# Two transformer layers on one core: half of a sequence's rows turned in 32x32 squares by VectorE and moved in SBUF, where TensorE turned them before

## The chip, the cores and the metric

The kernel runs on one core of a Trainium2 chip. The metric is the device time of one execution in microseconds (us). Four compute engines matter here: TensorE (PE, matmuls and transposes), VectorE (DVE), ScalarE (ACT) and GpSimd (POOL). SyncE (SP) issues most of the DMAs; ACT and POOL issue some as well. Matmul results land in PSUM, which the kernel uses as eight banks; everything else is in SBUF, with 128 partitions.

## The reference, cut to what matters

Two sequences (B=2) of 512 tokens with 512 features go through two layers, each an attention block and a feed-forward block. A residual is added and the rows are normalized after each block. The change lies between the first two blocks.

```python
# layer 0, attention: every fourth query head reads a memory M, normalized by z
q_sel = (elu(q) + 1)[:, :, ::4, :]                     # 8 heads of 128
num = einsum('bshd,hde->bshe', q_sel, M)
den = einsum('bshd,hd->bsh', q_sel, z)[..., None] + 1e-6
output = repeat(num / den, 4, axis=2).reshape(b, s, 4096) @ Wo.T
x = layernorm(x + output)                              # (M_new, z_new are not returned)
# layer 0, feed-forward: quantized, truncated to int8 twice; w_gate, w_up are ternary
gate, up = (x / 128) @ w_gate.T, (x / 128) @ w_up.T
inter_q = trunc(clip(silu(gate) * up * 128, -128, 127)).astype(int8)
x = layernorm(x + trunc(clip(inter_q @ w_down.T * 128, -128, 127)).astype(int8))
# layer 1: softmax attention, then a SwiGLU block of inner width 1376
x = layernorm(x + attention(x));  x = layernorm(x + swiglu(x))
```

## The kernel before

A sequence is cut into four tiles of 128 tokens; a tile has its tokens in the 128 partitions and 512 features along the row. The first block works in that layout. The feed-forward block contracts over the features, so it needs each sequence transposed: features in partitions, 512 tokens along the row, in four blocks of 128 features. It is needed in two parts, `xh` (a copy rounded to the matmul's input format, fp32r) and `xl` (what the rounding left), because each product of the block is taken with both parts.

The stage that the change touches is the loop over the eight tiles of both sequences, first (0,0) to (0,3) and then (1,0) to (1,3); step i handles `order[i]`. A step does this:

- `read(b, t)`: eight matmuls on PE (L557, tile `po`, one per head, each into its own PSUM bank). ACT takes the head's denominator from the last column (L561, `den`). DVE takes the reciprocal of four denominators at once (L565). The first three heads are scaled by ACT into SBUF tiles `y` (L570), which POOL adds up (L574). Heads 3 to 7 are scaled and added to the rows `x` by DVE (L579). Last, POOL adds the sum of the three to `x` (L586). A bank is free again when its head has been scaled.
- In the middle of `read`, `norm_a0(i - 1)` normalizes the tile before: statistics on DVE (L138, L140), a power on POOL (L146, L147), an offset on DVE (L664), and the final scaling on ACT (L665). So tile t is fully normalized in the middle of the step after it.
- `check_up`, `total`, `verdict`: steps that find whether the up weights are ternary, with a small matmul `pf_up` (L224) near the end.

After step 5 and after step 6, `block(k)` is called twice each: it transposes block k of all four tiles of the first sequence on PE (L275, four transposes of 128x128 into one PSUM bank `pt_f`), ACT copies the bank to `xh` (L280), and DVE subtracts to give `xl` (L281). The second sequence goes another way already: `turn_squares` lets DVE turn each normalized tile square by square, each square left where it stands (L671, a stream transpose into `squares`), and later `move_squares` sends each square to its place by 16 DMAs (L294): 9 from SP's queue, 4 from POOL's, 3 from ACT's. `split(1, xt1)` then makes `xh` and `xl` from the moved tile `xt_f`.

The order of instructions on PE, ACT, DVE and SP is set by a scheduler with a cost model when the program is built; `issue_after` ties single instructions to others. POOL's order alone is that of the code. PSUM tiles come from one pool of eight banks in turn, so a matmul waits for the reader of the tile eight places earlier. The large SBUF tiles of the stage come from pools: `pair_tile` gives one of four slots of 128x2x512 in pool `wop` (tag `wo`), which held the output weights until their sum was taken, and `xtp` has two slots of 128x4x512.

After the loop, the feed-forward block starts with the first sequence (L735), then the second.

Of the kernel before, what the change touches and what calls it, by code (L numbers as in the profile page):

```python
# [10 lines left out]
F32 = mybir.dt.float32  # L11
F32R = mybir.dt.float32r
# [7 lines left out]
P = 128  # L20
B, S, HID = 2, 512, 512
NT = S // P
NK = HID // P
# [16 lines left out]
def kernel(  # L40
# [19 lines left out]
    nc = tc.nc  # L60
# [6 lines left out]
    xtp = ctx.enter_context(tc.tile_pool(name="xtp", bufs=2))  # L67
# [14 lines left out]
    def psum(name):  # L82
        return ps.tile([P, 512], F32, tag="mm", name=name)


    xs = [[], []]
# [172 lines left out]
            wds.append(wd)  # L259
        return wds  # L260

    def split(b, xt=None):


        hi = xtp.tile([P, NK, S], F32, tag="xt", name=f"xh_{b}").bitcast(F32R)
        los = [pair_tile(f"xl_{b}_{i}").bitcast(F32R) for i in range(2)]
        his = [hi[:, k, :] for k in range(NK)]
        los = [los[k // 2][:, k % 2, :] for k in range(NK)]

        def block(k):  # L270
            h, l = his[k], los[k]
            if xt is None:
                rows = psum(f"pt_f0{b}_{k}")
                for t in range(NT):
                    nc.tensor.transpose(rows[:, ts(t, P)], xs[b][t][:, ts(k, P)], ident)  # L275
            else:
                rows = xt[:, :, k, :]
                h, l = (u.rearrange("p (t q) -> p t q", t=NT) for u in (h, l))
            return (
                nc.scalar.copy(h, rows),  # L280
                nc.vector.tensor_sub(l, rows, h.bitcast(F32)),  # L281
            )

        return his + los, block

    def move_squares(squares, xt):


        src = squares.rearrange("p t (k i) -> p (t k) i", k=NK)
        dst = xt.rearrange("p t k i -> p (t k) i")  # L290
        for i in range(P // SQ):
            for j in range(P // SQ):
                eng = nc.gpsimd if i == j else nc.scalar if i == (j + 2) % 4 > 0 else nc.sync
                dma = eng.dma_start(dst[ts(j, SQ), :, ts(i, SQ)], src[ts(i, SQ), :, ts(j, SQ)])  # L294
                if eng is nc.sync:
                    last = dma
        return last
# [4 lines left out]
    def pair_tile(name):  # L302
        return wop.tile([P, 2, HID], F32, tag="wo", name=name)
# [7 lines left out]
    def units(tile):  # L311
        return [tile[:, i, :] for i in range(tile.shape[1])]
# [66 lines left out]
    with tc.tile_pool(name="a0w", bufs=1) as a0w, tc.tile_pool(name="a0", bufs=2) as a0:  # L379
        wq = []  # L380
        for h in range(NH):
            if h % 2 == 0:
                two = query_tile(f"wq{h}").rearrange("p a (k d) -> p a k d", k=NK)
            w = two[:, h % 2]
# [163 lines left out]
        def read(b, t, between):  # L548

            x = xs[b][t]  # L550
            ys, steps = [], []
            for h0 in range(0, NH, 4):
                four = []
                den = small.tile([P, 4], F32, tag="den", name=f"den_{b}_{t}_{h0}")
                for j in range(4):
                    po = psum(f"po0_{b}_{t}_{h0 + j}")
                    nc.tensor.matmul(  # L557
                        po, qs[b][h0 + j][:, ts(t, P)], mw[:, h0 + j, :],
                        start=True, stop=True,
                    )  # L560
                    nc.scalar.activation(  # L561
                        den[:, j : j + 1], po[:, LAST:], AF.Identity, bias=den_eps
                    )
                    four.append(po)
                nc.vector.reciprocal(den, den)  # L565
                for j in range(4):
                    d = den[:, j : j + 1]
                    if h0 + j < LENT:
                        y = a0.tile([P, HID], F32, tag="y", name=f"y_{b}_{t}_{j}", bufs=3)
                        nc.scalar.activation(  # L570
                            y[:, :LAST], four[j][:, :LAST], AF.Copy, scale=d
                        )
                        if ys:
                            nc.gpsimd.tensor_add(  # L574
                                ys[0][:, :LAST], ys[0][:, :LAST], y[:, :LAST]
                            )
                        ys.append(y)
                    else:
                        steps.append(nc.vector.scalar_tensor_tensor(  # L579
                            x[:, :LAST], four[j][:, :LAST], d, x[:, :LAST], ALU.mult, ALU.add  # L580
                        ))
            between(steps)
            if (b, t) == order[-1]:
                steps.append(nc.vector.tensor_add(x[:, :LAST], x[:, :LAST], ys[0][:, :LAST]))
            else:
                nc.gpsimd.tensor_add(x[:, :LAST], x[:, :LAST], ys[0][:, :LAST])  # L586
            return steps
# [68 lines left out]
        def norm_a0(i, steps):  # L656

            b, t = order[i]
            with tc.issue_after(steps[1].ins):
                stats = layernorm_stats(xs[b][t], f"a0{b}_{t}")  # L660
            with tc.issue_after(steps[-1].ins):
                mv, rstd = stats
                off = small.tile([P, 1], F32, tag="off", name=f"off_{i}")
                nc.vector.tensor_scalar(off, mv[:, 0:1], rstd, -1.0, ALU.mult, ALU.mult)  # L664
            nc.scalar.activation(xs[b][t], xs[b][t], AF.Identity, bias=off, scale=rstd)  # L665

        x2 = []

        def turn_squares(i):
            b, t = order[i]  # L670
            nc.vector.transpose(squares[:, t, :], xs[b][t])  # L671

        for i, (b, t) in enumerate(order):
            steps = read(b, t, lambda steps: norm_a0(i - 1, steps) if i else None)
            for _ in range((1, 1, 1, 1, 1, 1, 0, 0)[i]):
                check_up(*checks.pop(0))
            if i == 5:
                tot_up = total(counts_up[0], "up")
            elif i == 6:
                flag_up, eff_up = verdict(tot_up, sc_up, "up")  # L680
            if i == 5:
                parts, block = split(0)
                x2.append(parts)
                squares = xtp.tile([P, NT, HID], F32, tag="xt", name="squares")
            if i in (5, 6):
                for k in range(2):
                    block(2 * (i - 5) + k)
            if i > NT:
                turn_squares(i - 1)
        norm_a0(len(order) - 1, steps)  # L690
        turn_squares(len(order) - 1)


# [10 lines left out]
        ]  # L704

    xt1 = fp.tile([P, NT, NK, P], F32, tag="it11", name="xt_f01", bufs=1)
    moved = move_squares(squares, xt1)
    wdp = ctx.enter_context(tc.tile_pool(name="wdp", bufs=1))
    with tc.issue_after(moved.ins):
        wds = down_weights(wd0_in, "0")  # L710
    with tc.tile_pool(name="f0", bufs=2) as f0:
# [134 lines left out]

        for c in range(LEAD - 2):
            up(0, c, [cut_off[f"f00_{c - 2}"]] if c > 1 else ())
        parts, block = split(1, xt1)
        x2.append(parts)  # L850
        moved = [ins for k in range(NK) for ins in block(k)]
        for c in range(LEAD - 2, LEAD):
            up(0, c, moved)
        for c in range(LEAD):
# [607 lines left out]
```

## Time and profile before

| | us |
|---|---|
| median of 3 runs | 459.4 |
| the runs | 459.14, 459.40, 459.92 |
| the profiled execution | 459.37 |
| its span in the trace | 457.6 |
| around the span | 1.77 |
| PE busy in the span | 449.9 |

The profile is of one execution. Its span runs from the first to the last instruction; the time outside it is the difference to that execution's own time. A row of a timeline gives the start from the span's start, the busy time of the group, the engine, the line of the kernel, the operation, output and inputs by name, shapes, a count, and in brackets the idle time before it and what ended it. Starts of neighbouring rows are more exact than durations on PE, since matmuls are pipelined and their ends are modelled.

### The profile page before, as it was taken

To read this page: it belongs to the slowest core of one execution; us is meant where nothing else is said; L and a number is where in the kernel's file an instruction comes from. 1 tells how busy PE (TensorE), PEld (TensorE's weight loads), DVE (VectorE), ACT (ScalarE), POOL (GpSimd) and SP (SyncE) were. 2 spreads that over 40 slices of the span, in tenths; PEclk is the share of its full clock that TensorE was granted. 3 is DMA by queue.
4 is the path that set the end of the run, shared out by engine and by line. 5 is a ranking of instruction groups with operands and counts; after the bars stand their busy time and mean duration, and the time that the engine had idled before them with its cause. 6 is when DMAs were issued, how large, how long until landed. Compare 5 with 4: busy or idle time off the path is not lost.

```text
span 457.6 us, 5879 instructions
## 1 busy us (share of the span) xinstructions
PE 449.9 (98%) x1929; PEld 338.0 (74%) x1929; DVE 339.5 (74%) x665; ACT 270.2 (59%) x514; POOL 110.5 (24%) x149
## 2 busy tenths in 40 slices
PE   8999999999999999999999999999999999999995
PEld 8887754344588888888766578888888888888884
DVE  4966757667867888847978899795656778998632
ACT  4778995556567975567748544564755658442101
POOL 0300206565550069101362332000000000050101
PEclk9999999999999999999999999999999999999999
DMA  8999980000038101131585500000000000001001
GB/s 293 392 267 313 178 319 1 0 3 0 2 51 238 55 3 48 47 93 38 199 323 92 94 0 2 0 0 1 0 1 0 1 1 0 1 23 46 34 37 47
DMA packets 28693, 37.14 MB, mean 81 GB/s; under 512 B 16304, under 2 KB 17200, under 8 KB 28656
## 3 DMA queue, kind: packets, MB, share of 16 engines
q1 hardware_dynamic: 23216, 30.13, 19.2%
q0 software_dynamic: 1984, 5.77, 6.8%
q10 hardware_dynamic: 3456, 0.75, 0.8%
q8 instruction: 22, 0.36, 0.3%
q14 instruction: 15, 0.12, 0.1%
HBM read 32.45 MB, written 2.10 MB: 75 GB/s over the span
## 4 chain that ended last, share of the span: by engine, by line
PE 92%; DVE 3%; issue 2%; DMA 1%; ACT 1%; SPq 0%; POOL 0%; POOLq 0%; DVEq 0%
PE pm L1252 17%; PE po L557 10%; PE pq L502 9%; PE pg_f L735 9%; PE pu_f L735 9%; PE pc L1252 8%; PE pdm L1340 8%; PE pd_f L794 4%; PE pdc L1340 4%; PE pqk L1063 3%; PE pv L1080 2%; PE pot L1129 2%; PE po L1146 2%; PE psc L1019 2%; PE pmw L543 2%
## 5 line engine op out<-in xcount | busy, mean ns | idle before, releaser
L557 PE MATMUL po<-mw,q 128*128 128x512 f32 x128 | 57.1, 599 | 0.7 <-ACT den L561 0.4
L557 PEld LDWEIGHTS po<-mw,q 128*128 128x128 f32 x128 | 22.9, 189 | 33.4 <-issue 18.6
L146 POOL TENSOR_TENSOR rstd_f<-mv_f,ln_eps 128x1 f32<-128x1 f32 x15 | 4.4, 295 | 170.8 <-DVE mv_f L1355 130.2
L1252 PE MATMUL pm<-r,ugu 128*128 128x512 f32 x152 | 37.7, 389 | 0.0
L1252 PE MATMUL pm<-r,it_early 128*128 128x512 f32 x144 | 36.6, 392 | 0.0
L1252 PEld LDWEIGHTS pm<-r,ugu 128*128 128x128 f32 x152 | 28.5, 188 | 5.9
L170 ACT ACTIVATE ta_f<-y_f,below_half 128x512 int8<-128x512 f32 (+1 forms) x22 | 15.8, 720 | 27.2 <-DVE y_f L158 26.9
L1252 PEld LDWEIGHTS pm<-r,it_early 128*128 128x128 f32 x144 | 27.0, 188 | 6.0 <-issue 0.5
L579 DVE SCALAR_TENSOR_TENSOR x<-po,den,x 128x511 f32<-128x511 f32 x40 | 29.8, 745 | 2.1
L1262 DVE SCALAR_TENSOR_TENSOR ev_q<-pm,ev_q 128x512 f32<-128x512 f32 x27 | 18.5, 686 | 14.2 <-PE pm L1252 12.0
L574 POOL TENSOR_TENSOR y<-y,y 128x511 f32<-128x511 f32 x16 | 21.1, 1320 | 25.5 <-PE po L557 20.6
L761 DVE SCALAR_TENSOR_TENSOR it_f<-tb_f,ta_f 128x512 fp32r<-128x512 int16 (+1 forms) x22 | 15.2, 690 | 13.8 <-ACT tb_f L171 13.8
L735 PE MATMUL pg_f<-xh,tu 128*128 128x512 f32 x88 | 24.4, 399 | 0.0
L1261 ACT ACTIVATE ev_q<-pc 128x512 f32<-128x512 f32 x27 | 16.0, 594 | 14.1 <-PE pc L1252 14.0
L735 PE MATMUL pg_f<-xl,tu 128*128 128x512 f32 x88 | 23.6, 389 | 0.0
L735 PE MATMUL pu_f<-xh,tu 128*128 128x512 f32 x88 | 23.5, 389 | 0.0
L735 PE MATMUL pu_f<-xl,tu 128*128 128x512 f32 x88 | 23.5, 389 | 0.0
L1142 ACT ACTIVATE x<-x,off_f,rstd_f 128x512 f32<-128x512 f32 x7 | 5.7, 816 | 27.7 <-POOL off_f L1141 27.7
L561 ACT ACTIVATE den<-po,den_eps 128x1 f32<-128x1 f32 x64 | 13.9, 277 | 12.8 <-PE po L557 12.7
L349 POOL TENSOR_SCALAR td<-wd,inv_down 128x512 fp32r<-128x512 f32 x11 | 20.1, 1847 | 1.6 <-DVE inv_down L206 1.6
L794 PE MATMUL pd_f<-td,it_f 128*128 128x512 f32 x88 | 20.3, 389 | 0.0
L1252 PE MATMUL pc<-r,ugu 128*128 128x512 f32 x72 | 19.3, 390 | 0.0
(368 smaller groups left out, 1142.7 us busy)
## 6 DMA issues: line engine op xcount, KB each, us to landing
gu<-in_gu SPq DMA_DIRECT2D x20, 512.0 KB, 6.9
wd<-in_wd SPq DMA_DIRECT2D x20, 256.0 KB, 4.2
wo<-in_wo SPq DMA_DIRECT2D x8, 512.0 KB, 8.7
wo<-in_wo POOLq DMA_DIRECT2D x8, 512.0 KB, 9.8
wq<-in_wq SPq DMA_DIRECT2D x8, 256.0 KB, 4.6
x<-in_x SPq DMA_DIRECT2D x7, 256.0 KB, 4.5
out<-x SPq DMA_DIRECT2D x7, 256.0 KB, 2.0
x<-in_bo POOLq DMA_DIRECT2D x4, 256.0 KB, 5.9
```

Source lines behind the costliest of these rows:

```text
L170: nc.scalar.activation(a[:n], y, AF.Relu, bias=below_half[:n])
L349: eng.tensor_scalar(out, w, factor, None, ALU.mult)
L502: done = nc.tensor.matmul(p, w, x, start=(start and i == 0), stop=(i == len(todo) - 1), skip_group_check=not start,)
L557: nc.tensor.matmul(po, qs[b][h0 + j][:, ts(t, P)], mw[:, h0 + j, :], start=True, stop=True,)
L574: nc.gpsimd.tensor_add(ys[0][:, :LAST], ys[0][:, :LAST], y[:, :LAST])
L579: steps.append(nc.vector.scalar_tensor_tensor(x[:, :LAST], four[j][:, :LAST], d, x[:, :LAST], ALU.mult, ALU.add))
L735: nc.tensor.matmul(pp[a], t[:, a, i % NK, :], x2[b][i], start=(i == 0), stop=(i == 2 * NK - 1),)
L794: nc.tensor.matmul(pd, inter[b][c][:, ts(t, P)], td[c].bitcast(F32R), start=(c == 0), stop=(c == last),)
L1252: nc.tensor.matmul(p, w, x, start=(left[id(p)] == begun[id(p)]), stop=(left[id(p)] == 1))
L1261: nc.scalar.activation(ev, pc, AF.Copy, scale=CROSS)
L1262: nc.vector.scalar_tensor_tensor(ev, pm, MAIN, ev, ALU.mult, ALU.add)
L1340: nc.tensor.matmul(p[:, :w], got[j // 4][1][kind][:, j % 4], down_parts[j][kind][:, cols], start=(j == 0 and kind == kinds[0]), stop=(j == ...
```

## The change

For the first sequence, tiles 0 and 1 no longer go through PE. Their normalized rows are turned in 32x32 squares by DVE after steps 1 and 2, into one half-size tile `squares_0`. 16 DMAs, all on SP's queue here (`three` is false), move the squares to `xt_f00`. At the start of step 5, one ACT copy of 128x1024 elements and two DVE subtractions of 128x512 make these tiles' parts of `xh` and `xl`; source and both results are in SBUF. Tiles 2 and 3 are still transposed by PE, tile by tile and not block by block: four transposes into one bank after step 4 (tile 2) and four after step 5 (tile 3), each followed by one ACT copy and two DVE subtractions of half the width. `squares_0` and `xt_f00` use two of the four `wo` slots, and the `xl` tiles of the second sequence take these slots over after them. The second sequence keeps its way and its counts; `split` is rewritten so that one function serves both.

```diff
--- before.py
+++ after.py
@@ -259,31 +259,35 @@
             wds.append(wd)
         return wds
 
-    def split(b, xt=None):
-
-
-        hi = xtp.tile([P, NK, S], F32, tag="xt", name=f"xh_{b}").bitcast(F32R)
-        los = [pair_tile(f"xl_{b}_{i}").bitcast(F32R) for i in range(2)]
-        his = [hi[:, k, :] for k in range(NK)]
-        los = [los[k // 2][:, k % 2, :] for k in range(NK)]
-
-        def block(k):
-            h, l = his[k], los[k]
-            if xt is None:
-                rows = psum(f"pt_f0{b}_{k}")
-                for t in range(NT):
-                    nc.tensor.transpose(rows[:, ts(t, P)], xs[b][t][:, ts(k, P)], ident)
-            else:
-                rows = xt[:, :, k, :]
-                h, l = (u.rearrange("p (t q) -> p t q", t=NT) for u in (h, l))
-            return (
-                nc.scalar.copy(h, rows),
-                nc.vector.tensor_sub(l, rows, h.bitcast(F32)),
+    def split(b):
+
+
+        hi = xtp.tile([P, NK, S], F32R, tag="xt", name=f"xh_{b}")
+        los = [wop.tile([P, 2, S], F32R, tag="wo", name=f"xl_{b}_{i}") for i in range(2)]
+
+        def tiles_of(t, n):
+            h, l0, l1 = (
+                u.rearrange("p k (t i) -> p k t i", t=NT)[:, :, t : t + n] for u in (hi, *los)
             )
 
-        return his + los, block
-
-    def move_squares(squares, xt):
+            def part(src, k=0, m=NK):
+                moved = [nc.scalar.copy(h[:, k : k + m], src)]
+                for i in range(0, m, 2) if m > 1 else (0,):
+                    w = min(m, 2)
+                    at = (k + i) % 2
+                    moved.append(
+                        nc.vector.tensor_sub(
+                            (l0, l1)[(k + i) // 2][:, at : at + w], src[:, i : i + w],
+                            h[:, k + i : k + i + w].bitcast(F32),
+                        )
+                    )
+                return moved
+
+            return part
+
+        return units(hi) + [u for lo in los for u in units(lo)], tiles_of
+
+    def move_squares(squares, xt, three=True):
 
 
         src = squares.rearrange("p t (k i) -> p (t k) i", k=NK)
@@ -291,6 +295,8 @@
         for i in range(P // SQ):
             for j in range(P // SQ):
                 eng = nc.gpsimd if i == j else nc.scalar if i == (j + 2) % 4 > 0 else nc.sync
+                if not three:
+                    eng = nc.sync
                 dma = eng.dma_start(dst[ts(j, SQ), :, ts(i, SQ)], src[ts(i, SQ), :, ts(j, SQ)])
                 if eng is nc.sync:
                     last = dma
@@ -665,12 +671,18 @@
             nc.scalar.activation(xs[b][t], xs[b][t], AF.Identity, bias=off, scale=rstd)
 
         x2 = []
+        half = pair_tile("squares_0"), pair_tile("xt_f00")
+        parts, tiles_of = split(0)
+        x2.append(parts)
+        squares = [half[0], xtp.tile([P, NT, HID], F32, tag="xt", name="squares_1")]
 
         def turn_squares(i):
             b, t = order[i]
-            nc.vector.transpose(squares[:, t, :], xs[b][t])
+            nc.vector.transpose(squares[b][:, t, :], xs[b][t])
 
         for i, (b, t) in enumerate(order):
+            if i == 5:
+                tiles_of(0, 2)(half[1].rearrange("p t (k i) -> p k t i", k=NK))
             steps = read(b, t, lambda steps: norm_a0(i - 1, steps) if i else None)
             for _ in range((1, 1, 1, 1, 1, 1, 0, 0)[i]):
                 check_up(*checks.pop(0))
@@ -678,15 +690,16 @@
                 tot_up = total(counts_up[0], "up")
             elif i == 6:
                 flag_up, eff_up = verdict(tot_up, sc_up, "up")
-            if i == 5:
-                parts, block = split(0)
-                x2.append(parts)
-                squares = xtp.tile([P, NT, HID], F32, tag="xt", name="squares")
-            if i in (5, 6):
-                for k in range(2):
-                    block(2 * (i - 5) + k)
-            if i > NT:
+            if i in (4, 5):
+
+                pt = psum(f"pt_f00_{i - 2}")
+                for k in range(NK):
+                    nc.tensor.transpose(pt[:, ts(k, P)], xs[0][i - 2][:, ts(k, P)], ident)
+                tiles_of(i - 2, 1)(pt.rearrange("p (k t i) -> p k t i", k=NK, t=1))
+            if i in (1, 2) or i > NT:
                 turn_squares(i - 1)
+            if i == 2:
+                move_squares(half[0], half[1].rearrange("p t (k i) -> p t k i", k=NK), False)
         norm_a0(len(order) - 1, steps)
         turn_squares(len(order) - 1)
 
@@ -704,7 +717,7 @@
         ]
 
     xt1 = fp.tile([P, NT, NK, P], F32, tag="it11", name="xt_f01", bufs=1)
-    moved = move_squares(squares, xt1)
+    moved = move_squares(squares[1], xt1)
     wdp = ctx.enter_context(tc.tile_pool(name="wdp", bufs=1))
     with tc.issue_after(moved.ins):
         wds = down_weights(wd0_in, "0")
@@ -846,9 +859,11 @@
 
         for c in range(LEAD - 2):
             up(0, c, [cut_off[f"f00_{c - 2}"]] if c > 1 else ())
-        parts, block = split(1, xt1)
+        parts, tiles_of = split(1)
         x2.append(parts)
-        moved = [ins for k in range(NK) for ins in block(k)]
+        moved = []
+        for k in range(NK):
+            moved += tiles_of(0, NT)(xt1[:, :, k : k + 1, :].rearrange("p t k i -> p k t i"), k, 1)
         for c in range(LEAD - 2, LEAD):
             up(0, c, moved)
         for c in range(LEAD):
```

## The prediction

> **What bounds the kernel now.** I read the page first: shares, slices, chain. Times are us from the span's start.
>
> ```profile
> span 457.6 us, 5879 instructions
> ...
> PE 449.9 (98%) x1929; PEld 338.0 (74%) x1929; DVE 339.5 (74%) x665; ACT 270.2 (59%) x514; POOL 110.5 (24%) x149
> ...
> PE   8999999999999999999999999999999999999995
> ...
> PE 92%; DVE 3%; issue 2%; DMA 1%; ACT 1%; SPq 0%; POOL 0%; POOLq 0%; DVEq 0%
> ```
>
> PE is busy 98% and carries 92% of the chain; its clock is 0.998. Time is gained by giving PE less work, or lost by making it wait. The changed stage is 85 to 122 us: steps i=4 to 7 of the loop over tiles. PE's timeline there:
>
> ```profile
> 104.86 1.04 PE L275 MATMUL pt_f<-ident,x 128*128 128x128 f32 x8
> 105.78 1.98 PE L557 MATMUL po<-mw,q 128*128 128x512 f32 x4
> 108.12 1.10 PE L557 MATMUL po<-mw,q 128*128 128x512 f32 x2 [0.36 <-ACT den L561]
> 109.37 4.53 PE L557 MATMUL po<-mw,q 128*128 128x512 f32 x10 [0.15 <-DVE mv_a L140]
> ...
> 113.88 1.07 PE L275 MATMUL pt_f<-ident,x 128*128 128x128 f32 x8
> 114.79 2.82 PE L557 MATMUL po<-mw,q 128*128 128x512 f32 x6
> 117.76 4.53 PE L557 MATMUL po<-mw,q 128*128 128x512 f32 x10 [0.15 <-DVE mv_a L140]
> ```
>
> Each head's read is two matmul passes, 0.859 together where nothing waits (62.82 to 104.86 holds 48 at 0.876). The x8 rows are the transposes, 105.78-104.86 = 0.92 and 0.91: 1.83 in all, on the path. The rows that begin late show PE waiting for a PSUM bank. Head 2 of i=6 is 0.5 late; head 3 starts 1.25 after head 2, 0.39 late; head 3 of i=7 likewise. With some 0.1 more, PE loses 1.4 here. After 122 PE has no gap until 230, so what is won or lost here passes on one for one.
>
> The late banks are freed by DVE, VectorE's timeline:
>
> ```profile
> 106.95 0.18 DVE L565 RECIPROCAL den<-den 128x4 f32<-128x4 f32 x1 [2.28 <-ACT den L561]
> 107.23 0.75 DVE L579 SCALAR_TENSOR_TENSOR x<-po,den,x 128x511 f32<-128x511 f32 x1
> ...
> 109.23 0.66 DVE L281 TENSOR_TENSOR xl<-pt_f,xh 128x512 fp32r<-128x512 f32 x1
> ```
>
> Head 2 starts at 108.12, 0.89 after the L579 that frees its bank starts: the rule I use below.
>
> **The change part by part.**
>
> PE: 8 of the 16 transposes go. A transpose is spaced 0.92/8 = 0.115, so half of 1.83 goes: -0.92, all on the path. Tile 2 is turned between i=4 and 5, tile 3 between i=5 and 6.
>
> VectorE turns: two stream transposes, 0.71 each (the L671 row of the second sequence). Tile 0's normalized rows are ready near 83.4, tile 1's near 90.8 (ACT L665 of tile 1 is 89.89 for 0.81). DVE idles 2.30 before 85.74 and 2.12 before 92.92: both are hidden, +0. Without that idle each would cost up to 0.71.
>
> Here the Trainium skill speaks against the change. "VectorE: DVE Perf Modes", The three transpose paths: VectorE can give only a grid of 32x32 blocks; its rules advise TensorE where a PSUM result will do. The trace agrees on the bare price: PE turns a tile in 4 x 0.115 = 0.46, VectorE in 0.71 plus eight of the 16 moves. Summed in series the rule makes this a loss; in this trace the turns stand in idle time, so I take -0.92 and look at the moves.
>
> Moves: 16 DMAs of 32x8x32, all issued by SP. SP stands still from 62.8 to 132.3, waiting for the second sequence's squares; the 16 are put ahead of that wait, so they delay no load.
>
> ```profile
> SPq L294 <- DVE squares L671: 69.5, 1, 69.5
> ...
> L294 SPq DMA_DIRECT2D xt_f<-squares x9: 627/747/1009, 132.4 to 139.0; - x9
> ...
> DMA to landing us min/median/max: 2.1/3.1/4.5
> ```
>
> Eight intervals from 132.4 to 139.0 are 0.82 each, with ACT's and POOL's queues beside; the last ones, alone, 0.63 long. From a first issue at 91.65, fifteen intervals of 0.68 end at 101.9, and with 2.1 to 3.1 landing it is 104.0 to 105.0. At 0.82: 103.95 and 106.0 to 107.0. The copy can start at 106.0 (below). I take the former, as this queue is alone and each move is half as large: hidden, with 1 to 2 us of slack.
>
> ACT and DVE in i=5 and 6: four copies 128x512 (L280) become one 128x1024 and two 128x512; four subtractions of 512 become two of 512 (tiles 0,1) and four of 256. ACT's copy spaces 0.466 for 512, y (L570) 0.57; I take 0.82 for 1024 with 0.98 to its end (estimate: proportional, less one fixed part). A 256 subtraction is 0.31 (estimate, half of 0.58 to 0.60 plus overhead).
>
> The walk. PE: tile 2's transposes 98.3 (normalized at 98.19), 0.3 late; i=5 head 0 at 98.7, head 7 at 104.9; tile 3's transposes 105.7; i=6 head 0 at 106.17, 1 at 107.03, 2 at 107.89. DVE has tile 2's two subtractions beside its i=5 reads, and ACT's L665 of tile 3 moves from 103.76 to 104.12. Then ACT: y0 104.84, y1 105.41, the 1024 copy 106.0 to 107.0, y2 106.8 to 107.5. The big subtractions stand in DVE's order before the second reciprocal of i=5 and x heads 4 to 7; DVE stands idle for this copy from 105.0 to 107.05. Queued behind the wait are exactly the L579s whose banks PE needs for heads 3, 4, 5 and 7 of i=6.
>
> Without anything else: subtractions 107.05 and 107.65, reciprocal, x4 at 108.5. Head 3 then starts at 109.33 (0.6 late), head 4 at 110.65 (0.46), 5 at 111.71 (0.2), head 7 at 113.42; i=7 starts at 114.42 against 114.79. i=7 has no subtraction left to delay it, so its 0.39 also goes: its end is -0.78. That is the whole ledger: -0.92 transposes, +0.1 tile 2's and other small waits, stalls 1.3 for 1.4.
>
> **The shared port, the term that decides.** The new subtractions read both inputs from SBUF (xt_f and xh); the old ones read one from PSUM. What happens beside a POOL add is shown earlier:
>
> ```profile
> 69.70 0.74 DVE L211 SCALAR_TENSOR_TENSOR junk<-t,sc_up,gu 128x512 int8<-128x512 f32 x1
> ...
> 70.55 1.56 DVE L211 SCALAR_TENSOR_TENSOR junk<-t,sc_up,gu 128x512 int8<-128x512 f32 x1
> ...
> 69.87 3.37 POOL L574 TENSOR_TENSOR y<-y,y 128x511 f32<-128x511 f32 x2 [20.55 <-PE po L557]
> ```
>
> A compare with two SBUF inputs takes 0.75 elsewhere. POOL's first add, asked for during the first compare, ran once that ended; the second compare took 1.56, until the add was over; then the second add waited for it. Both adds together 3.37 against 2.63 undisturbed. The Trainium skill says it in "SBUF — State Buffer", Who interferes with whom: a VectorE instruction with two SBUF inputs and a GpSimd one reading SBUF exclude each other, the later one fully blocked. It speaks against the change, and the trace agrees: 1.56 for 0.75.
>
> Here: the first add (y1) runs 106.16 to 107.43 and holds the first subtraction back by about 0.25, to 107.3. The second add is ready when y2 is, 107.58, while that subtraction runs; it takes the port at its end, near 107.8, for its 1.27 (undisturbed half of 2.62). The second subtraction starts near 108.95 and ends near 109.5; x4 starts at 109.7. Head 3 then starts at 110.6 (1.8 late), 4 at 111.9, 5 at 113.0, 7 at 114.7. i=7 starts at 115.68 instead of 114.79 and wins back 0.39 by not stalling. Its end: +0.48. So the sum is -0.78 without the rule, +0.48 with it. Below, no contention gives -0.78; above, both subtractions held a full 1.27 give about +1.0. I take +0.48, the nearest row being full-width adds that got in between two such DVE operations.
>
> Other order changes on DVE, ACT and POOL are swaps of single small operations, covered by PE's work after 122; at most 0.2 either way if that cover is gone.
>
> **The rivals.**
>
> A, the port stays out of it: the second subtraction starts before the add, or the overlap is harmless. For: y2 and that subtraction are only 0.3 apart, and in a later place two DVE operations with two SBUF inputs met tiny POOL ones with no loss to DVE. Against: the 1.56 above. Result -0.78, with the small delay of the first subtraction alone -0.6: 458.6 to 458.8. Its stalls hang on the 1024 copy: each 0.1 that it is shorter gives 0.1 more, so a shorter copy takes it past -0.92.
>
> B, late moves: SP's issue at 0.82 or more, or landings of 4.5. It decides once the last landing passes 106.0; ACT then waits with its copy, and y2, den of i=6 and DVE's second half behind it. Landing at 108 puts the copy 2 us later, of which PE's banks absorb some: about +1.2, 460.6. For: 0.82 in the measured stretch. Against: no other queue here. This one is slower.
>
> C, it doesn't do what it says: the tiles 2 and 3 are still turned on PE, so half a gain is built in; that the 0.92 isn't on the path is excluded by the PE rows.
>
> **How the numbers follow.** The profiled execution is 459.37 (457.6 span, 1.77 around it), 0.03 under the median 459.40 of 459.14 to 459.92. Forecast: 459.37+0.48 = 459.85, chance 0.46; its own range 459.3 to 460.6, from the walk's estimates (copy, port handover) of some 0.6 each way. A 0.36; B 0.18. C takes nothing. A measurement of this kernel can tell about 0.2%, 0.92 us, from no change. Forecast: 0.02 faster, 0.31 same, 0.13 slower. A: 0.18, 0.18, 0 (-0.92 is 0.14 past its sum, and a copy shorter than my estimate takes stalls with it). B: 0, 0.01, 0.17. Sums: faster 0.20, same 0.50, slower 0.30. The range reaches from A's 458.6 less 0.2 to B's 460.6 plus 0.4: 458.4 to 461.0.
>
> **What would show it.** PE: 8 L275-like transposes fewer, 0.46 per tile; turns of tiles 0 and 1 in DVE's idle at 83 and 91; SP's last move issued near 102. For the forecast: the second xt_f subtraction takes about 1.6 to 1.9 instead of 0.68, with a POOL add between, and head 3 of i=6 near 110.6. For A: both subtractions near 0.68 and i=7 from 114.4. For B: ACT's 1024 copy starting after 106.5 with a DMA as its releaser. I am wrong if PE stalls elsewhere after 122, or if i=6 has no stall at all (then about -1.9).

## The result, and the profile after

| | before | changed |
|---|---|---|
| median of 6 runs, us | 459.41 | 461.55 |
| lowest to highest | 459.14 to 459.92 | 461.16 to 462.04 |
| span of the profiled execution | 457.6 | 459.7 |

The ratio is 1.0045, interval 1.0034 to 1.0056: slower by 2.1 us (1.6 to 2.6), where 0.5 was forecast. In a later comparison (f1 below) the same kernel stood at 1.0025 (1.0016 to 1.0034), so the loss is 0.2 to 0.6%, and its size is not the same in each comparison.

The page of the changed kernel, its first rows:

```profile
span 459.7 us, 5888 instructions
...
PE 450.6 (98%) x1921; PEld 337.6 (73%) x1921; DVE 342.6 (75%) x669; ACT 270.4 (59%) x513; POOL 106.7 (23%) x149
...
PE 90%; DVE 3%; issue 2%; ACT 2%; DMA 1%; POOL 0%; SPq 0%; POOLq 0%; ACTq 0%; DVEq 0%
```

Shares and busy times hardly moved; a loss of 2 us in 459 has to be read from its stage. PE's timeline there (start, busy time, what it runs, and in brackets the idle time before the row):

```profile
98.74 0.66 PE L697 MATMUL pt_f<-ident,x 128*128 128x128 f32 x4
99.23 7.54 PE L563 MATMUL po<-mw,q 128*128 128x512 f32 x16
106.61 0.60 PE L697 MATMUL pt_f<-ident,x 128*128 128x128 f32 x4
107.04 2.74 PE L563 MATMUL po<-mw,q 128*128 128x512 f32 x6
111.49 1.13 PE L563 MATMUL po<-mw,q 128*128 128x512 f32 x2 [1.70 <-DVE x L585]
112.83 3.87 PE L563 MATMUL po<-mw,q 128*128 128x512 f32 x8 [0.22 <-DVE mv_a L140]
116.53 0.28 PE L224 MATMUL pf_up<-tot_up,ones 128*128 128x1 f32 x2
116.67 7.11 PE L563 MATMUL po<-mw,q 128*128 128x512 f32 x16
123.24 1.48 PE L748 MATMUL pg_f<-xh,tu 128*128 128x512 f32 x4
```

The transposes are 4 and 4, where the kernel before has 8 and 8. Head 3 of i=6 is the row at 111.49, with a wait of 1.7 ahead of it that DVE's read ends. Step i=7 (116.67) has no wait left. DVE and POOL, from their timelines:

```profile
105.11 0.75 DVE L585 SCALAR_TENSOR_TENSOR x<-po,den,x 128x511 f32<-128x511 f32 x1
107.88 2.61 DVE L279 TENSOR_TENSOR xl<-xt_f,xh 128x512 fp32r<-128x512 f32 x2 [2.03 <-ACT xh L274]
110.41 0.16 DVE L571 RECIPROCAL den<-den 128x4 f32<-128x4 f32 x1
110.68 0.75 DVE L585 SCALAR_TENSOR_TENSOR x<-po,den,x 128x511 f32<-128x511 f32 x1
```

```profile
107.00 1.27 POOL L580 TENSOR_TENSOR y<-y,y 128x511 f32<-128x511 f32 x1 [0.85 <-ACT y L576]
108.58 1.36 POOL L580 TENSOR_TENSOR y<-y,y 128x511 f32<-128x511 f32 x1 [0.32 <-ACT den L567]
```

And the moved tile's own view, 85 to 130 us (duration min/median/max in ns; of two, these are the first and the second):

```profile
L300 SPq DMA_DIRECT2D xt_f<-squares x16: 598/608/748, 92.0 to 101.9; - x16
L279 DVE TENSOR_TENSOR xl<-xt_f,xh x2: 934/1342/1749, 107.9 to 108.7; 128x512 fp32r<-128x512 f32 x2
...
DMA to landing us min/median/max: 1.9/1.9/2.3
```

The two subtractions take 0.93 and 1.75, together 2.61. POOL's second addition (108.58 to 109.94) begins just before the first one is over, and the second one ends 0.55 after that addition. The moves are done by 101.9 + 2.3 = 104.2, 2.6 before the copy at 106.81: they were hidden.

How far PE has fallen behind the profile of before, by the start of the same matmul in both: 0.5 when the reads of i=0 begin, still 0.5 at the end of i=4, 1.52 when the feed-forward block begins (123.24 against 121.72), and 2.09 from 148 us on. So there are three pieces: 0.5 at the start, +1.02 in the stage, +0.56 near 145. In what follows, "the stage" is this shift between the start of i=2 and the start of the feed-forward block (up to the end of i=4 nothing moves here; the runs below that turn tiles 0 and 1 on PE do it from the end of i=2 on); "the second split" is the shift around 145, where the block takes up the second sequence.

The third piece, PE's timeline at 145 and ACT's ahead of it, in the changed kernel, and then ACT's two rows in the kernel before:

```profile
145.43 1.45 PE L748 MATMUL pg_f<-xh,tu 128*128 128x512 f32 x4
146.72 1.22 PE L748 MATMUL pg_f<-xl,tu 128*128 128x512 f32 x4
```

```profile
133.85 2.77 ACTq L300 DMA_DIRECT2D xt_f<-squares  x3
136.66 0.72 ACT L170 ACTIVATE ta_f<-y_f,below_half 128x512 int8<-128x512 f32 x1 [3.01 <-issue]
...
144.17 2.17 ACT L274 CAST xh<-xt_f 128x512 fp32r<-128x512 f32 x4
```

```profile
132.27 2.11 ACTq L294 DMA_DIRECT2D xt_f<-squares  x3
...
141.93 2.17 ACT L280 CAST xh<-xt_f 128x512 fp32r<-128x512 f32 x4
```

A group of four matmuls takes 1.07 elsewhere. ACT's three issues took 2.11 before and 2.77 here. The copies came at 141.93 and 144.17, which is 0.7 more than PE's own 1.52. PE lost 0.56 of that, so the copies had some 0.15 to spare before (an estimate, from these two numbers).

### The profile page after: what moved, and what is told of

It is laid out like the page before. It is cut to its first block, busy times and chain, and to the rows that moved or that the text cites. A ratio compares the mean times of both kernels' runs of the same rounds, so it can differ in the third digit from the quotient of the medians.

```text
span 459.7 us, 5888 instructions
## 1 busy us (share of the span) xinstructions
PE 450.6 (98%) x1921; PEld 337.6 (73%) x1921; DVE 342.6 (75%) x669; ACT 270.4 (59%) x513; POOL 106.7 (23%) x149
## 4 chain that ended last, share of the span: by engine, by line
PE 90%; DVE 3%; issue 2%; ACT 2%; DMA 1%; POOL 0%; SPq 0%; POOLq 0%; ACTq 0%; DVEq 0%
PE pm L1267 17%; PE pq L508 9%; PE pg_f L748 9%; PE pu_f L748 9%; PE po L563 8%; PE pc L1267 8%; PE pdm L1355 8%; PE pd_f L807 4%; PE pdc L1355 4%; PE pqk L1078 3%; PE pv L1095 2%; PE pot L1144 1%; PE po L1161 1%; PE psc L1034 1%; PE pmw L549 1%
```

## The experiments

Times are compared with runs of the kernel before, next to each other on the same chip. "Subtractions" is the time of the two on xt_f. The stage and the second split are those of one profiled execution, against the profile of before.

| run | ratio (95%) | stage, us | subtractions, us | second split, us |
|---|---|---|---|---|
| changed, the result | 1.0045 (1.0034, 1.0056) | +1.02 | 2.61 | +0.56 |
| f1 changed again | 1.0025 (1.0016, 1.0034) | +1.00 | 2.61 | 0 |
| e1 no additions | 1.0017 (1.0008, 1.0025) | -0.31 | 1.29 | 0 |
| g3 first addition only | 0.9992 (0.9980, 1.0005) | -0.09 | 1.53 | 0 |
| e2 copy first | 0.9999 (0.9987, 1.0012) | -0.49 | 1.29 | 0 |
| e3 both later | 1.0013 (1.0004, 1.0023) | -0.30 | 1.28 | +1.59 |
| e4 PE, tile by tile | 1.0002 (0.9990, 1.0014) | -0.52 | none | 0 |
| f3 the same and moves | 1.0002 (0.9993, 1.0011) | -0.13 | none | +1.00 |
| h1 the same and turns | one execution | -0.13 | none | 0 |
| f2 second moves on POOL | 1.0040 (1.0025, 1.0055) | +0.99 | 2.60 | 0 |
| f4 copy first, moves on POOL | 0.9994 (0.9982, 1.0006) | -0.46 | 1.29 | 0 |
| g2 after x head 3 | 1.0017 (1.0002, 1.0031) | -0.25 | 0.93, 1.56 | +1.33 |
| h2 and turn behind | 0.9991 (0.9979, 1.0002) | -1.41 | 1.53 | +0.78 |
| h3 and moves on POOL | 0.9983 (0.9972, 0.9994) | -1.41 | 1.53 | 0 |
| k2 h3 again | 0.9995 (0.9985, 1.0006) | -1.44 | 1.53 | +1.74 |
| k1 before, moves on POOL | 1.0004 (0.9993, 1.0015) | 0 | none | 0 |
| g1 before again | 0.9997 (0.9987, 1.0006) | 0 | none | 0 |

The stage repeats within 0.05 (changed twice and f2: 1.02, 1.00, 0.99; h2, h3, k2: -1.41, -1.41, -1.44). The ratios scatter more: e1, whose stage is 0.2 better than that of g3, has the worse ratio by 0.0025, and the two intervals do not overlap. What e1's other executions lost is not in its one trace. So the stage is read from the traces, and the ratios say what is left of it at the end.

**e1, the additions left out.** In `read`, ahead of the POOL addition:

```diff
-                        if ys:
+                        if ys and (b, t) != (1, 1):
```

> The changed kernel, with POOL's two additions of the three y tiles of tile (1,1) left out (the part of the sum that they make is missing); everything else as in the changed kernel. Theory 'port': these additions hold the port that the two subtractions xl<-xt_f need; without them the two take 1.3 us together instead of 2.6, head 3 of step i=6 is late by 0.5 instead of 1.8, and the time falls by 1.3 from 461.5 to about 460.2. Theory 'queue': DVE's wait for the 1024-wide copy costs it all, the additions nothing: 461.5 as before. Theory 'moves': the DMAs in SBUF slow the subtractions: they stay at 2.6 and the time at 461.5.

The subtractions, in the tile's view of this run:

```profile
L279 DVE TENSOR_TENSOR xl<-xt_f,xh x2: 684/688/691, 107.7 to 108.4; 128x512 fp32r<-128x512 f32 x2
```

1.29 in place of 2.61, as theory 'port' said, and the stage is 1.33 shorter. DVE's queue still waits 2.03 for the copy, so 'queue' alone is out; the moves are the same, so 'moves' is out. The ratio fell from 1.0045 (1.0025 in f1) to 1.0017; against f1 that is 0.4 us and not the 1.3 forecast, with intervals that overlap. The times of e1 alone leave the lock's price open; its trace shows it.

**g3, only the second addition left out.**

```diff
-                        if ys:
+                        if ys and (b, t, j) != (1, 1, 2):
```

> The changed kernel with only the second of POOL's two additions of tile (1,1) left out (y2's part of the sum is missing). Theory 'gets in between': the second addition alone, asked for during the first subtraction, costs the 1.0; without it the two xt_f subtractions take some 1.6 together (the first held 0.3 by the first addition), against 2.6 with both additions and 1.3 with none, and the time is about 1.0 below the changed kernel. Theory 'the first addition': they stay near 2.6.

```profile
L279 DVE TENSOR_TENSOR xl<-xt_f,xh x2: 678/804/931, 108.8 to 109.7; 128x512 fp32r<-128x512 f32 x2
```

The first subtraction keeps its 0.93, the second falls from 1.75 to 0.68. So the first addition costs 0.25 and the second 1.07: it was asked for while the first subtraction ran and went in between the two. The ratio is below f1's by 0.0033, 1.5 us, more than the stage's 1.1, but with no overlap of the intervals.

**f1, the changed kernel again.** No edit.

> The changed kernel itself, once more, beside the others of this call. If the loss of 0.45% is the kernel's and not that one session's, it is 1.6 to 2.6 above the kernel before again, with the second xt_f subtraction near 1.75, head 3 of i=6 1.8 late, and some wait of PE at the second sequence's split near 145.

Stage and subtractions are the same as in the result, to 0.02. The second split has no wait this time: ACT's three issues took 2.36 and the copies came in time. So the wait expected there did not come, and the loss is 0.7 to 1.6 and not 1.6 to 2.6. The ratio, 1.0025, is about what a stage of 1.00 gives (0.0022).

**e2, the copy ahead of y0.** Ties of order alone (the lines are shortened):

```diff
+                first_half = tiles_of(0, 2)(half[1]...)           # at i == 5
...
+                            if (b, t) == (1, 1):                  # around ACT's y, and den heads 5 to 7
+                                tied.enter_context(tc.issue_after(first_half[0].ins))
```

> The changed kernel, with the 1024-wide copy xh<-xt_f put ahead of y0 of tile (1,1) on ACT instead of after y1 (two ordering ties, no work changed). The last move was issued at 101.9 and should have landed by 104.0, the copy can start near 105.0. Theory 'port and queue': the subtractions then run 106.0 to 107.3, in time in which DVE stood idle and before the first addition (near 107.2): 0.68 each, head 3 of i=6 waits 0.3 at most, the time falls by 2.0 to 2.4, to 459.1 to 459.5. Theory 'moves': the copy waits for its DMAs and starts at 106 or later all the same: about 461. If y0 to y2, now 1 us later, hold PE's banks up, heads 0 to 2 of i=6 start late and the gain is halved: 460.4.

ACT's timeline and DVE's row in this run:

```profile
106.48 1.03 ACT L274 CAST xh<-xt_f 128x1024 fp32r<-128x1024 f32 x1
107.41 1.83 ACT L582 ACTIVATE y<-po,den 128x511 f32<-128x511 f32 x3
```

```profile
107.54 1.29 DVE L279 TENSOR_TENSOR xl<-xt_f,xh 128x512 fp32r<-128x512 f32 x2 [0.88 <-ACT xh L274]
```

The subtractions are done at 108.8, when POOL's first addition starts (108.74). No wait of 1.7 is left; 1.5 of the stage comes back and the kernel is level with before. y0 holds head 0 of i=6 up by 0.3, the smaller part of the last theory.

**e4, without squares.** The calls of `tiles_of(0, 2)` and `move_squares` and the first two turns are dropped, and

```diff
-            if i in (4, 5):
+            if i in (2, 3, 4, 5):
```

> The changed kernel without squares and moves for the first sequence: all four tiles are turned by PE, tile by tile, after steps i=2, 3, 4 and 5, each with one copy and two half-width subtractions from PSUM. 16 transposes as before the change (1.83 us on PE), no subtraction with two SBUF inputs in this stage. Theory 'port and queue': the loss of the changed kernel was in the SBUF subtractions, so this is near the kernel before, 459.0 to 459.8, with the stalls of i=6 and i=7 (1.4) spread out or gone. Theory 'tile by tile': the small extra waits that tile 2's subtractions caused in i=5 (0.44 in the trace) come four times: 460.5 to 461.

Level, with a stage of -0.52: turning tile by tile, which the change brought along, costs nothing and saves some of the stalls. The small waits of a tile's subtractions are there (0.2 in i=5), but do not come to 1 us.

**f3, e4 with the turns and moves done and unused; h1, with the turns alone.**

> All four tiles turned by PE tile by tile, as in the run without squares, and beside that the turns and the 16 moves of tiles 0 and 1 are done as in the changed kernel, their result unused. Theory 'hidden': the same time as without them, at most 0.3 more, since VectorE turns in idle time and SP has nothing else to do. Theory 'moves disturb': the reads x head 4 of i=5 begin 0.36 late again, as in each run with the moves, SP's queue starts the second moves differently, and ACT's issues take longer: 0.5 to 1.5 more than without.

> All four tiles turned by PE tile by tile, and VectorE turns tiles 0 and 1 in squares as in the changed kernel, but nothing is moved (the squares are unused). In each run with the 16 moves, DVE began x head 4 of tile (1,0), in step i=5, 0.64 after the reciprocal ahead of it, and 0.28 after it in the kernel before and in the run without squares. Theory 'moves': without the moves it is 0.28 again. Theory 'turns' (the two more instructions in DVE's stream): 0.64 as with them.

f3's ratio is e4's. But its stage lost 0.39 against e4, and h1 loses the same without a single move: in the stage the turns cost this and the moves nothing. In all runs with the two turns DVE starts x head 4 of tile (1,0) 0.64 after the reciprocal ahead of it, in e4 and before 0.28. In the changed kernel, and then in e4:

```profile
100.11 0.18 DVE L571 RECIPROCAL den<-den 128x4 f32<-128x4 f32 x1 [1.94 <-ACT den L567]
100.75 0.75 DVE L585 SCALAR_TENSOR_TENSOR x<-po,den,x 128x511 f32<-128x511 f32 x1 [0.46 <-DVE den L571]
```

```profile
101.34 0.18 DVE L571 RECIPROCAL den<-den 128x4 f32<-128x4 f32 x1 [2.13 <-ACT den L567]
101.62 0.75 DVE L585 SCALAR_TENSOR_TENSOR x<-po,den,x 128x511 f32<-128x511 f32 x1
```

In the changed kernel heads 4 and 5 of i=5 then start 0.23 and 0.20 late on PE. No wait in the program explains it. It comes with the two added DVE instructions and not with the moves. In each of these runs the late read is the 192nd record of DVE's queue, waits counted; in e4 and before the same read is the 190th. So it goes by the position in the queue (more on this in the last section); why that position starts late stays open.

**e3, both later.** The call of `tiles_of(0, 2)` at `i == 6` in place of `i == 5`.

> The changed kernel, with the copy and the two subtractions of tiles 0 and 1 called one step later (at the start of i=6 instead of i=5): on DVE they now come after x heads 4 to 7 of tile (1,1), on ACT after y2. Theory 'port and queue': the reads that PE waits for are no longer behind them, heads 3 to 7 of i=6 wait 0.2 at most, and the time falls to 458.8 to 459.4, whatever the subtractions meet on the port. Theory 'port alone': the subtractions are still slow beside an addition of i=6, and what they hold back is only later: about 460.5.

No read of i=6 waits, as 'port and queue' said, but the time is not the 458.8 to 459.4 forecast. This run's PE row, POOL's and those of DVE read:

```profile
115.17 0.38 PE L224 MATMUL pf_up<-tot_up,ones 128*128 128x1 f32 x2 [0.86 <-ACT y L576]
```

```profile
112.41 2.37 POOL L592 TENSOR_TENSOR x<-x,y 128x511 f32<-128x511 f32 x1 [1.13 <-DVE x L585]
```

```profile
112.37 1.28 DVE L279 TENSOR_TENSOR xl<-xt_f,xh 128x512 fp32r<-128x512 f32 x2
113.57 0.70 DVE L681 STREAM_TRANSPOSE squares<-x 128x512 f32<-128x512 f32 x1
114.20 0.13 DVE L571 RECIPROCAL den<-den 128x4 f32<-128x4 f32 x1
```

POOL's addition took 2.37 in place of 1.27, since this time DVE was first with its subtractions: the same lock, the other way round. The addition was asked for during the first subtraction and yet did not get in between the two, unlike in the changed kernel. PE's 0.86 does not come from this addition: PE waits for ACT's first y, which begins at 114.43, before the addition ends (114.78). ACT's row has that y waiting 0.68 for DVE's reciprocal, and the reciprocal (114.20) stands behind the two subtractions and the turn. The stage still gains 0.30; 1.59 is then lost at the second split.

**f2 and f4, the second sequence's moves without ACT.**

```diff
+                if three == 2 and eng is nc.scalar:
+                    eng = nc.gpsimd
...
-    moved = move_squares(squares[1], xt1)
+    moved = move_squares(squares[1], xt1, 2)
```

> The changed kernel, with the three moves of the second sequence that ACT issues given to POOL's queue. Theory 'second wait': in the changed kernel ACT's three issues took 2.7 instead of 2.0, what ACT does next came 0.65 later, and PE waited 0.5 at the second split; without them on ACT that wait is gone and the time is 0.5 or more below the changed kernel. Theory 'moves late': the second split waits for the landings and not for ACT: no gain, or a loss as POOL's seven moves end later.

> Both repairs together: the 1024-wide copy ahead of y0 on ACT, and the second sequence's three ACT moves on POOL's queue. If the two losses are separate, this is the changed kernel less 2 less 0.5: 0.3 to 0.8 below the kernel before. If the copy's place was all, it is the same as with the copy moved alone, level with the kernel before.

Neither gains. The wait at the second split is not there in the profiles, but it was not there in f1 either, and f2's ratio is not below that of f1. 'Second wait' as a steady part of the loss is not borne out: it comes in some executions. f4 is level, as e2.

**g2, the subtractions in DVE's idle time of i=6.** The copy is called at the start of i=6, the subtractions behind `issue_after(steps[0].ins)`, which is x head 3.

> The changed kernel, with the 1024-wide copy after the y tiles of (1,1) (called at the start of i=6) and the two xt_f subtractions on DVE only after x head 3 of i=6, in DVE's idle time of that step. Theory 'port and queue': no read of i=6 waits for them and POOL's additions of i=6 may delay them without harm to PE; the later call before this stalled PE 0.9 at pf_up as a subtraction held POOL's addition of x up, and this avoids that. PE loses only 0.3 for tile 2, 0.4 in i=5 and some 0.5 in i=6; the stage ends 0.9 to 1.4 before that of the kernel before, 458.3 to 458.9 beside 459.4. Rival: what waits at the start of the feed-forward block for xl, or what POOL does later (rstd, y), takes the gain back: level with before.

PE was 1.36 ahead by the middle of i=7, as forecast for it, and then lost 1.1 again, so the 0.9 to 1.4 forecast did not come. DVE's rows (113.48 and 114.97) have the turn of tile (1,0) between the two, POOL's addition got in there, and the second took 1.56; the next reciprocal came at 117.59 and the read behind it at 117.79, too late for heads 4 and 5 of i=7. A further 1.33 went at the second split.

**h2 and h3, the turn behind both; h3 with the moves on POOL.**

```diff
+                with tc.issue_after(subs[-1].ins):
+                    turn_squares(4)                               # at i == 6; no longer at the end of i == 5
```

> As the run with the subtractions after x head 3 of i=6, but the second subtraction comes right behind the first and the turn of tile (1,0) after both. There the turn stood between them, a POOL addition got in, the second took 1.56 and the next reciprocal came at 117.8, which cost 1.1 of the 1.36 won by then. Theory 'port': now both are done before that addition is ready (0.93 and 0.68), the reciprocal comes near 116.4, i=7 has no wait, and the stage ends 1.2 to 1.4 before that of the kernel before: 0.2 to 0.3% faster. Rival: the turn or the verdict's small operations come late instead, or the second sequence's split waits for ACT: level, or slower by 0.1%.

> The same, and the second sequence's three ACT moves on POOL's queue. If the wait at the second split (1.0 to 1.5 in those profiles in which ACT's third move took over 1.4) is what takes the gain, this one has none and is 0.2 to 0.3% faster than the kernel before; if it is only chance between executions, it equals the run without this.

h3's PE timeline, from the tile 3 transposes to the feed-forward block, and DVE's row:

```profile
106.61 0.60 PE L704 MATMUL pt_f<-ident,x 128*128 128x128 f32 x4
107.04 7.24 PE L565 MATMUL po<-mw,q 128*128 128x512 f32 x16
114.12 0.28 PE L224 MATMUL pf_up<-tot_up,ones 128*128 128x1 f32 x2
114.26 7.11 PE L565 MATMUL po<-mw,q 128*128 128x512 f32 x16
120.81 1.50 PE L755 MATMUL pg_f<-xh,tu 128*128 128x512 f32 x4
```

```profile
113.27 1.53 DVE L279 TENSOR_TENSOR xl<-xt_f,xh 128x512 fp32r<-128x512 f32 x2
```

There is no wait in brackets between 106.61 and 120.81, and the stage ends 1.41 ahead of before. h3 is the fastest kernel seen here: 0.9983 (0.9972, 0.9994). h2 lost 0.78 at the second split, where ACT's three issues took 3.10, and 1.0 more at 223 us, where the second layer begins; that one also differs between executions (0.8 in k1, 0.2 in h3).

**k1 and k2.** The queue alone on the kernel before, and h3 once more.

> The kernel before, with only the second sequence's three ACT moves given to POOL's queue. If the gain of the best run (0.17%) came from the queue and not from the squares of the first sequence, this shows it too: ratio 0.998. If it came from the stage at 98 to 122 us, which ended 1.34 earlier there, this is level: 0.9995 to 1.001.

> The best run once more, beside it: squares of tiles 0 and 1, subtractions after x head 3 of i=6, the turn behind them, the second moves on POOL. Theory: 0.2 to 0.3% below the kernel before, with the stage ending 1.3 earlier and no wait at the second split. Rival: the first result was chance: level.

The queue alone gives nothing. k2 has the same stage as h3, but its ratio is 0.9995, and its profile shows where 1.74 went. ACT's waits from 128 to 150 us in k2 (total, times, longest):

```profile
ACT ta_f L170 <- DVE y_f L158: 4.7, 4, 1.5
ACT xh L274 <- DMA xt_f<-squares: 2.3, 1, 2.3
```

With PE 1.4 earlier, the copies of the second sequence wait for their moves to land. One of SP's issues took 2.13 there; in h3 the longest was 1.91. So the gain of the stage is shown, and that it reaches the end is not sure: the two comparisons of the same kernel together stand for about 0.1%.

**g1, the kernel before again.** No edit.

> The kernel before, unchanged, for a second profile of it. Each kernel of this study but the profiled execution of before has its transposes at 5 to 7 us at half pace for 1 to 2 us longer (0.4 to 0.5 later by 10 us). Theory 'chance': this is an execution's own start, so this profile of before may show it too, and the time is that of before, ratio 1.000. Theory 'systematic': before starts early here as well.

Its span is 459.1, not 457.6. It too has its first transposes at half pace, 0.21 apart up to 5.9 us, and is 0.4 behind by then (0.2 when the reads begin). By the start of i=2 PE loses 1.2 more, waiting for ACT's y and DVE's x; ACT had stood 1.1 for a load of gate weights, which it does not in the profile of before. And f1, the changed kernel, begins its reads 0.2 before the profile of before. So theory 'chance' holds: the 0.5 at the start of the profile after is the execution's and not the change's.

## Why the prediction was wrong

- **The term that decides.** Right in kind and size. Expected: an addition between the two subtractions, the second 1.6 to 1.9; measured 1.75. The first was to be held 0.25; it took 0.93 for 0.68. Head 3 of i=6 was put at 110.6; it came at 111.0, the 0.5 of the start taken off. e1 and g3 take both blockings away one by one. The rule of the Trainium skill ("SBUF — State Buffer", Who interferes with whom) holds here in both directions, by 1.75 for 0.68 on DVE and 2.37 for 1.27 on POOL. That the addition would get in between the two was taken from one earlier row. It did so in the changed kernel, f1 and f2, but not in e3, so this part had some luck.
- **"Both are hidden, +0", of the turns.** This step failed. DVE does turn the tiles in its idle time, but with the two turns x head 4 of (1,0) starts 0.36 late, two reads of i=5 wait 0.43 in place of 0.1, and everything behind moves: the normalization of tile 3 began at 104.46 (less the 0.5) and not at 104.12, the copy at 106.31 and not at 106.0. e4 and h1, without and with the turns, differ by 0.39 in the stage.
- **The 1024 copy and the pair.** The copy was estimated at 0.98 to its end; it took 1.04. From the first subtraction's start to the read behind the pair the walk has 2.65 (107.05 to 109.7), the trace 2.80 (107.88 to 110.68). Together 0.2 more. The stage: 0.48 forecast, +0.3 from the late copy and +0.2 make 1.0; measured 1.02.
- **The ledger.** Its sum does not close: -0.92, +0.1 and 1.3 for 1.4 make -0.92, not -0.78. The 0.3 by which the walk itself starts tile 2's transposes late is missing from the list. The walk, from which the forecast was taken, has it.
- **"What is won or lost here passes on one for one."** Wrong at the second split. PE has no gap there before, but the copies of the second sequence were on time with some 0.15 to spare. In the profile after 0.56 was lost there, in f1 nothing, and where PE came earlier (k2) 1.74.
- **The moves (rival B) and the PE saving.** The moves were done 2.6 before they were needed, at 0.66 from issue to issue (0.68 forecast). Turning by PE stays at 4 + 4, as said. Summed in series, the rule of the Trainium skill that advises TensorE ("VectorE: DVE Perf Modes", Rules for kernel authors) made this a loss. In the stage the moves cost nothing (f3 against h1), but the turns cost 0.39 by the late read (h1 against e4). h3's stage, 0.89 ahead of e4's, shows that the gain on PE is real all the same.
- **The sum.** Of the profile's 2.1, the stage's 1.02 is the change's each time, the second split's 0.56 comes and goes, and 0.5 is the start of the one execution shown of before. The medians of the first comparison differ by 2.1 too; of that only 1.02 is explained as steady, and f1's 1.0025 agrees with it. The kernel's loss was 1.6 to 2.6 in the first comparison and 0.7 to 1.6 in the second. Stage and second split together, 1.58, reach just the range's top of 461.0; what carried all six executions beyond it is not shown, since only one of them was profiled.

## What to carry to other kernels

When data that was read from PSUM is moved to SBUF, look at what becomes of the operand: a two-input VectorE operation that gains a second SBUF input now shares a lock with a GpSimd addition near it (here 1.75 us for 0.68), and what is queued behind it on VectorE pays for it. Put such operations where GpSimd has nothing ready (e2: 0.69 and 0.68), with nothing between them (g2: 1.56) and nothing urgent behind them. An instruction in idle time is not free by that alone: look at what moves behind it. A gain in one stage of a kernel that is 98% bound by one engine arrives only if the next just-in-time hand-over has slack too; find that hand-over before counting one for one.

## What the runs showed of the hardware that had not been expected

- A DVE read in PSUM started 0.36 later, in every run with two more DVE instructions ahead of it (14 of 14, each with 0.64 from reciprocal to read), and not in e4 or before. Over all 18 profiles DVE stood idle 19 times for more than 0.13 where nothing but its own work was ahead. All 19 idle times stand before a record whose number in DVE's queue is a multiple of 64 (records in order of start, waits counted): the 192nd in the 14, the 320th once (e4), the 832nd in f2, f4, h3 and k2. The cause is open.
- A POOL addition asked for during the first of two DVE subtractions in a row went in between them in the changed kernel, f1 and f2 (the second took 1.75), and waited for both in e3 (2.37 for 1.27). What decides it is not shown.
- Sixteen moves of 32x8x32 on one queue ran at 0.66 from issue to issue in the changed kernel (0.66 to 0.74 over the runs) and landed after 1.9 to 2.3; when two or three queues issued the second sequence's moves of twice the size, the longest single issue took 1.0 to 1.1 in before, g1 and k1 and 1.3 to 2.1 in the 15 others (e4 and h1 too, which move nothing for the first sequence), on SP or on ACT, differently from one execution to the next (ACT's third: 0.66 in f1, 1.07 in the result, 1.64 in g2). Of the 13 profiles in which ACT issues moves, the five in which its third took over 1.0 are the five with a loss at the second split. All five also move squares of the first sequence (5 of 9 that do, 0 of 4 that do not); whether the change brings this wait on is not settled by so few.
- The first transposes run 0.21 apart at first and 0.11 later, at a granted clock that the profiles put at 1.00 throughout; the pace changes between 4.0 and 7.2 us, from one execution to the next (5.05 in the one of before that the prediction used, 6.1 in g1), worth 0.4 to 0.5 us there.
